# Two of three PReLUs with one ScalarE pass each, and small sums at the ends of PSUM banks, in a fused convolution and attention kernel

## The chip, the cores and the metric

The kernel runs on one core of a Trainium2 chip. A core has five engines that work from queues of their own: TensorE (PE, the matrix multiplier), VectorE (DVE), ScalarE (ACT), GpSimd (POOL) and SyncE (SP), which here issues the DMA transfers. TensorE writes only to PSUM, a small memory of eight banks of 512 fp32 columns on each of 128 partitions. In this kernel VectorE and ScalarE read and write both PSUM and SBUF, and POOL works on SBUF alone. The metric is the time on the device in microseconds (us); lower is better. A profile also records when each instruction ran on each engine.

## What is computed

Input `x` is (16, 256, 56, 56) in fp32. There are two layers, each added to its own input, and each starts with a group norm over 32 groups. Cut to what matters:

```python
# layer 0, on _gn(x)
xq = sign(x + bias)
for i, d in enumerate((1, 3, 5)):                  # three dilations, 4 channel groups
    wq = scale_i * sign(w[i] - mean(w[i]))         # one scale per output channel: mean |w|
    y = conv3x3(xq, wq, dilation=d) + cb[i] - move1[i]
    y = where(y >= 0, y, alpha[i] * y)             # PReLU, one alpha per channel
    out = out + y + move2[i]
out = (out - mean_c(out)) * rsqrt(var_c(out) + eps) * gamma + beta   # over the 256 channels
x = x + out
# layer 1, on _gn(x): 8 heads, 9 neighbours of each pixel
q, k_in, v_in = qkv(x)
k = unfold3x3(k_in) + dcb + dwconv(k_in) + rpb     # v likewise, without rpb
x = x + proj(softmax(q . k over the 9) . v)
```

## The kernel before

The 16 images are worked on one after another, with the stages of neighbouring images overlapping. An image is cut into two strips (`u` = 0, 1), and a strip is held as tiles of 128 partitions by 784 columns (`UNIT`): 64 channels of the upper and 64 of the lower half of the image stand on the partitions. The 256 channels make four groups `g` of 64. So `conv` (line 706) is called 24 times an image: 2 strips x 4 groups x 3 dilations `d`.

**One convolution.** 36 matmuls (line 716) fill one pair of PSUM banks, columns 0 to 391 of each. Then a PReLU is taken from the pair and summed into the strip's tile `ct`. With `c` the sum in PSUM, `s` the weight scale and `b` the bias, PReLU is `alpha*(s*c + b) + (1 - alpha)*relu(s*c + b)`. The part `alpha*s*c` is written or added first: by ScalarE into `ct` for the first dilation (line 735, with the constant `mv2` as its bias), by VectorE into `ct` for the second (line 745), by ScalarE into a tile `rl` for the third (line 742). ScalarE then takes the Relu in place in PSUM (line 750), and VectorE adds `oalpha` times it to `ct` or `rl` (line 755). For the third dilation, POOL at last adds `rl` to `ct` (line 761). The scalars per channel are `asc` (`alpha*s`), `csc` (`s`), `cbi` (`b`) and `oalpha` (`1 - alpha`); `asc` and `csc` are written by `keep` (line 1220) as the weights are prepared, the others by `vectors` (line 1114).

**The channel norm.** `channel_norm` (line 793) squares `ct` on ScalarE (799), sums `ct` and its square over the channels on TensorE (769, in `lanes_sum`, with the constant matrix `cm32`), works out mean and root in small steps (813 to 821), spreads them back by TensorE (783), subtracts the mean (827) and multiplies by the root (837) on VectorE, adds the result to `xt` on POOL (850), and squares again on ScalarE (854) for the second group norm.

**Small sums.** `group_stats` (line 572) serves both group norms: one small matmul chain (587) and some nine small steps on VectorE and ScalarE (599 to 607) in a PSUM pair `gp`. `fold` (866) scales the qkv weights by the result and forms the biases `bf` by small matmuls (884) in a pair `bp`.

**The attention.** qkv (matmuls 906, ScalarE evictions 924); nine products of `q` with shifted rows of `k` (line 959, on POOL or VectorE) into tiles `p`; ten matmul groups (980) that sum them to the scores; the softmax on VectorE and ScalarE (1009 to 1031); for each of nine neighbours a matmul group (1044), a VectorE step (1055) into a tile `m` and a POOL add (1070), and a last VectorE step (1075); the projection (1087) and its VectorE add into `xt` (1097); then the store (1107).

**Who goes first.** Instructions are not issued in the order of the loops. The class `Plan` (line 368) collects them as `Op`s. Each has a place: `PERIOD` times the image, plus a number from the table `ORDER`, which has a row for each stage (`conv0` is strip 0's convolutions; `$` marks the last image's rows, `^` the first's). `Plan.emit` goes by rising place and takes the first operation whose inputs were issued and whose buffers are free; each engine then works through its own queue in that order, and waits where its next instruction's inputs aren't ready. `ON_VECTOR` lists the operations of `either` that VectorE does instead of POOL. The number of buffers of a kind bounds how far the order can run ahead: 4 pairs of PSUM banks (`ps`), 8 `ct`, 1 `rl`, 7 `p`, 4 `m`.

Of the kernel before, what the change touches and what calls it, by code (L numbers as in the profile page):

```python
# [34 lines left out]
LANES = 32  # L35
SCALE = (C // NH) ** -0.5
# [36 lines left out]
class Op:  # L73
    def __init__(self, place, emit, bufs):
# [6 lines left out]
PERIOD = 1231  # L81
ORDER = {
    "conv0": (
        -682, -410, -359, -2832, -303, -327, -265, -333, -280, -264, -245, -1566, -289, -213, -969, -970,
        -319, -128, -2067, -24, -3260, -58, -18, -16, -1028, -3936, 5, 17, 18, 101, 198, -321, 208, -3768,
        197, 207, 182, -601, -3937, 20, -15, -19, -199, 30, -146, 111, -2560, 21, -394, -20, -152, -3331,
    ),
    "conv0$": (
        -685, -409, -2692, -2836, -277, -2837, -419, -253, 194, -189, 109, -866, -1791, -207, -131, -440,
        -4781, -30, -3248, 99, -154, -250, -557, -386, -2111, -2366, 32, -462, -149, -2080, 175, -1794,  # L90
        -2185, -2439, 121, 140, -6017, -1732, -220, -9, -641, 100, -155, 112, -1493, 147, -1733, 191, 240,
        149, -865, -2379,
    ),
    "conv0^": (
        -2099, -6338, -223, -5746, -1337, -3215, -66, -5779, -1241, -202, -65, -5786, -1673, 42, -67, -667,
        -358, 124, 92, 358, -3217, 123, 231, 234, -3216, 565, 167, 400, 401, -1668, 228, 318, 504, -54, 229,
        -13, 515, -1726, -288, 227, 402, -115, -71, 40, -72, 517, -1182, 702, -116, -769, -2031, 119,
    ),
    "conv1": (
        160, -122, -123, 185, 199, -740, 209, -834, 265, -287, 150, -2506, -1087, 320, 171, 170, -823, 333,  # L100
        -2428, 361, -1220, 326, -175, 180, -1339, 356, 319, 255, 254, -2493, 355, -1340, 394, -1221, 714,
        746, 632, -113, -2040, 412, -162, -296, -1322, 470, -3611, 514, -1195, 925, -1683, -2369, 905, -1995,
    ),
    "conv1$": (
        56, -644, -645, -1492, 306, -11476, -498, -11477, 418, 239, 237, -3613, 188, 148, 146, 190, -1497,
        248, -878, 152, -867, 292, 151, -2181, -2390, -2392, 192, 98, 66, -864, 773, -432, 813, -1612, 662,
        456, 455, -1613, -818, 419, -28, -29, 44, 774, -431, 816, -434, 953, 968, 284, 678, -660,
    ),
    "conv1^": (
        666, 513, 523, -1198, 726, -697, -757, 826, 776, 581, 725, 830, 871, 682, 522, 601, -2033, 828, 824,  # L110
        695, 832, 829, 724, 578, 835, 715, 711, 612, 609, -2032, 865, 831, 878, 811, 949, 902, 901, 1044,
        1106, 38, 717, 718, 827, 869, 815, 890, -2027, 922, -1136, -964, 940, 959,
    ),
    "first^": (-3247,),
    "fold": (
        1404, -2035, -892, -2087, -3779, -4755, -952, -4221, -7223, -9967, -564, -942, -953, 1414, -949,
        -562, 1455, 407,
    ),
    "fold$": (
        1238, 1089, 753, 927, 1174, 593, 772, 1298, 934, 929, 595, 268, 1484, 297, 648, 1286, 559, -6518,  # L120
    ),
    "fold^": (
        1395, -941, -2847, -582, -784, 793, 792, -861, -863, -1498, -846, 1074, 1037, 696, 1424, -847, 1481,
        1444,
    ),
    "load0": (310,),
    "load0$": (539,),
    "load0^": (744,),
    "load1": (771,),
    "load1$": (614,),  # L130
    "load1^": (-117,),
    "mean0": (
        301, -2124, -1860, -2389, 172,
    ),
    "mean0$": (
        336, 87, 139, -232, -216,
    ),
    "mean0^": (
        785, 930, 214, -4431, 979,
    ),  # L140
    "mean1": (
        719, 911, 1038, -307, 787,
# [218 lines left out]
    "scale0^": (10,),  # L361
    "scale1$": (4,),
    "scale1^": (4,),
    "value0^": (4,),
}


# [1051 lines left out]
```

## Time and profile before

| | before |
|---|---|
| median of 3 runs | 1863.83 us (1862.01 to 1864.88) |
| the profiled execution: its own time | 1872.31 us |
| its span, first to last instruction | 1870.5 us |
| mean granted TensorE clock | 0.979 |
| instructions | 62125 |
| DMA | 217.03 MB, mean 116 GB/s |
| busy in the first 34 us: PE, DVE, ACT | 10.12, 28.93, 13.17 us |

Times in the profile are in us unless marked ns. Engines: PE is the matmul, PEld the load of its weights, which overlaps it. In a row of a group, after the line, the engine and the operation come the names (output <- inputs), the shapes, the count, and after a bar the busy time with the mean of one in ns, and then the idle time of the engine just before them, with what ended it. A row of waits says who waited for whom, for how long in total, how often, and the longest. The chain of work that ended last is followed back from the last instruction: at each step to what released it, or to the instruction before it on its engine. An idle engine that isn't the bottleneck costs nothing.

### The profile page before, as it was taken

Reading aid. Unit: us, or ns where it says so; the run is one execution under the profiler, and the core shown is the slowest. Engines: PE = TensorE matmul, PEld = TensorE weight load, DVE = VectorE, ACT = ScalarE, POOL = GpSimd, SP = SyncE. Lnnn points to the kernel's source line nnn. Section 1 sums busy time; section 2 is a strip of 40 time slices with the busy share of each in tenths; the row PEclk is TensorE's granted clock in tenths of the full one; section 3 lists DMA queues with packets and bytes.
Section 4 is the critical chain, followed back from the end, with each engine's and each line's share of the span. In section 5 each row is a group of like instructions: output and inputs, shape, how many; then the busy total and the mean of one; then the engine's idle time right before and its main releaser. Section 6 shows DMA issues by size and latency. Waiting matters only on the chain.

```text
span 1870.5 us, 62125 instructions
## 1 busy us (share of the span) xinstructions
PE 1653.7 (88%) x27322; PEld 953.1 (51%) x27322; DVE 1570.8 (84%) x2217; ACT 1314.6 (70%) x1861; POOL 1408.7 (75%) x782
## 2 busy tenths in 40 slices
PE   4879899898999989898998989899898989989784
PEld 3546455454545545454554545455454545745341
DVE  8777979979797997979799797979979797997966
ACT  5988778677777867677786777778677787755320
POOL 2147769688686968868696886869688686967865
PEclk9799999999999999999999999999999999999897
DMA  7852655547475554647555464755547467223023
GB/s 178 200 113 43 143 123 122 126 93 155 96 158 111 124 126 92 149 102 155 115 120 124 96 151 101 156 113 124 123 94 150 101 147 172 62 69 74 11 61 69
DMA packets 102094, 217.03 MB, mean 116 GB/s; under 512 B 10816, under 2 KB 84672, under 8 KB 101568
## 3 DMA queue, kind: packets, MB, share of 16 engines
q1 hardware_dynamic: 101824, 213.06, 51.8%
q8 instruction: 214, 3.51, 0.8%
q14 instruction: 56, 0.46, 0.1%
HBM read 156.23 MB, written 51.38 MB: 111 GB/s over the span
## 4 chain that ended last, share of the span: by engine, by line
PE 53%; POOL 18%; DVE 16%; issue 6%; ACT 4%; DMA 1%; SPq 0%; POOLq 0%; DVEq 0%; ACTq 0%
PE banks L716 19%; POOL m L1070 13%; PE banks L906 12%; PE banks L980 9%; DVE m L1055 4%; PE banks L1044 3%; PE banks L769 3%; POOL xt L850 3%; PE banks L1087 2%; ACT banks L750 2%; DVE rl L755 2%; DVE ct L755 2%; POOL p L959 1%; POOL ct L761 1%; DVE m L1075 1%
## 5 line engine op out<-in xcount | busy, mean ns | idle before, releaser
L716 PE MATMUL banks<-sgn,wconv 64*64 64x392 bf16 x13824 | 656.7, 335 | 60.3 <-DVE m L1055 25.8
L716 PEld LDWEIGHTS <-wconv 64*64 64x64 bf16 x13824 | 442.8, 106 | 279.1 <-issue 94.7
L1070 POOL TENSOR_TENSOR m<-m 128x784 f32<-128x784 f32 x255 | 475.3, 1864 | 95.9 <-DVE m L1055 82.2
L959 POOL TENSOR_TENSOR p<-qt,kt 128x784 f32<-128x784 f32 x267 | 468.1, 1789 | 93.2 <-ACT qt L924 88.0
L750 ACT ACTIVATE banks<-banks,cbi,csc 128x784 f32<-128x784 f32 x384 | 370.3, 973 | 95.8 <-DVE ct L745 95.8
L761 POOL TENSOR_TENSOR ct<-ct,rl 128x784 f32<-128x784 f32 x125 | 233.3, 1866 | 252.7 <-DVE ct L755 147.8
L1044 PE MATMUL banks<-at,wv 64*64 64x392 f32 x2560 | 276.1, 510 | 56.5 <-DVE lv L821 22.6
L1055 DVE SCALAR_TENSOR_TENSOR m<-banks,vb,vt 128x784 f32<-128x784 f32 x288 | 289.6, 1022 | 25.4 <-POOL m L1070 17.6
L755 DVE SCALAR_TENSOR_TENSOR ct<-banks,oalpha,ct 128x784 f32<-128x784 f32 x256 | 258.1, 1026 | 17.1 <-ACT banks L750 16.4
L906 PE MATMUL banks<-xt,wf 64*64 64x392 f32 x3072 | 269.0, 491 | 0.0
L850 POOL TENSOR_TENSOR xt<-xt,ct 128x784 f32<-128x784 f32 x124 | 229.2, 1871 | 1.4 <-DVE ct L837 1.3
L980 PE MATMUL banks<-p,wk 64*64 64x392 f32 x2304 | 213.7, 489 | 2.8 <-POOL p L959 2.6
L742 ACT ACTIVATE rl<-banks,asc 128x784 f32<-128x784 f32 x128 | 116.7, 912 | 107.0 <-PE banks L716 103.0
L906 PEld LDWEIGHTS banks<-xt,wf 64*64 64x64 f32 x3072 | 131.2, 133 | 101.2 <-issue 68.3
L643 ACT ACTIVATE xh<-xh 128x1568 f32<-128x1568 f32 x120 | 180.6, 1507 | 0.7
L735 ACT ACTIVATE ct<-banks,mv,asc 128x784 f32<-128x784 f32 x128 | 128.5, 1004 | 73.0 <-PE banks L716 72.8
L755 DVE SCALAR_TENSOR_TENSOR rl<-banks,oalpha,rl 128x784 f32<-128x784 f32 x128 | 131.8, 1030 | 53.6 <-ACT banks L750 48.8
L1044 PEld LDWEIGHTS banks<-at,wv 64*64 64x64 f32 x2560 | 86.8, 134 | 176.3 <-issue 69.2
L745 DVE SCALAR_TENSOR_TENSOR ct<-banks,asc,ct 128x784 f32<-128x784 f32 x128 | 131.0, 1024 | 24.9 <-PE banks L716 21.3
L980 PEld LDWEIGHTS banks<-p,wk 64*64 64x64 f32 x2304 | 93.1, 133 | 93.4 <-issue 76.2
L854 ACT ACTIVATE ct<-xt,pr 128x784 f32<-128x784 f32 x128 | 120.2, 940 | 25.4 <-POOL xt L850 23.0
L1087 PE MATMUL banks<-m,wp 64*64 64x392 f32 x1024 | 106.4, 518 | 32.1 <-DVE m L1075 29.6
(115 smaller groups left out, 1870.6 us busy)
## 6 DMA issues: line engine op xcount, KB each, us to landing
xh<-in_x SPq DMA_DIRECT2D x248, 392.0 KB, 5.7
xt<-in_x SPq DMA_DIRECT2D x128, 392.0 KB, 9.2
out<-xt SPq DMA_DIRECT2D x128, 392.0 KB, 5.9
sgn<-sgn SPq DMA_DIRECT2D x128, 41.2 KB, 7.6
p<-in_w SPq DMA_DIRECT2D x12, 144.0 KB, 3.2
xt<-in_wk_parts SPq DMA_DIRECT2D x1, 1344.0 KB, 8.1
xt<-in_wv_parts SPq DMA_DIRECT2D x1, 1280.0 KB, 9.4
wq<-in_wqkv SPq DMA_DIRECT2D x1, 384.0 KB, 9.7
```

The costliest lines, as they stand in the source:

```text
L643: lambda func=func, col=col: nc.scalar.activation(inside(g) if b == 0 else image(xh), image(xh), func, accum_out=sums[:, col : col + 1]),
L716: nc.tensor.matmul(out=ps[q * GC : (q + 1) * GC, h, 0:SN], lhsT=wconv[h * GC : (h + 1) * GC, g, d, tap, :], rhs=sgn[g][h * GC : (h + 1) * ...
L750: lambda: nc.scalar.activation(n(), n(), AF.Relu, bias=cbi[:, g, s], scale=csc[:, g, s]),
L755: lambda: nc.vector.scalar_tensor_tensor(to.tile, n(), oalpha[:, g, s], to.tile, ALU.mult, ALU.add),
L761: lambda e: e.tensor_tensor(ct.tile, ct.tile, to.tile, ALU.add),
L850: lambda e, g=g: e.tensor_tensor(xt[:, g], xt[:, g], ct[g].tile, ALU.add),
L906: nc.tensor.matmul(out=ps[h * D : (h + 1) * D, q, 0:SN], lhsT=wf[q * GC : (q + 1) * GC, g, j, :], rhs=xt[q * GC : (q + 1) * GC, g, h, :], ...
L959: e.tensor_tensor(p.tile.rearrange("p x (r w) -> p x r w", w=W), _view(qt[:, 0, u * SN :], [(NU * SN + LANES, 2), (W, SR), (1, W)]), shift ...
L980: nc.tensor.matmul(out=ps[q * D : (q + 1) * D, h, 0:n], lhsT=wk[r, j, :], rhs=rhs, start=s == 0, stop=s == 9,)
L1044: nc.tensor.matmul(out=ps[h * D : (h + 1) * D, q, 0:SN], lhsT=wv[q * D : (q + 1) * D, j, :], rhs=at[q * D : (q + 1) * D, h, 0:SN], start=True,
L1055: lambda j=j, m=m, ps=ps: nc.vector.scalar_tensor_tensor(m.tile.rearrange("p x (r w) -> p x r w", w=W), _view(ps[:, 0, :], [(512, 2), (W, ...
L1070: lambda e, m=m, acc=acc: e.tensor_tensor(acc.tile, acc.tile, m.tile, ALU.add),
```

## The change

For the first and third dilation the size of `1 - alpha` now goes into the Relu's scale and bias. `keep` and `vectors` prepare other scalars: `rsc` in place of `csc` (for these two dilations multiplied by that size), and `sgd`, which is +1 or -1 by the sign of `1 - alpha`. ScalarE takes one Relu pass from PSUM straight into SBUF, and VectorE adds `asc` times the PSUM pair to it. The second dilation keeps its three passes. For the third, ScalarE then makes a pass inside SBUF that brings in `mv2` and the sign; for the first, the sign is brought in later, by the matrix `cms` in the channel sum and by the mean subtraction (line 827), which takes a scalar with it. `rl` has two buffers.

The small sums `gp` and `bp` get a buffer kind of their own, `few`: columns 470 to 511 of the second bank of each pair. All eight banks are now one PSUM tile, and buffers are views of it, handed out in the order in which they came free. The POOL add at 1070 gets a view by rows of its tiles. `ORDER`, `PERIOD` and `ON_VECTOR` have new values throughout.

```diff
+TAIL = 470
-PERIOD = 1231
+PERIOD = 1207
 ORDER = {
...
-    "load1": (771,),
+    "load1": (237,),
...
     "stats": (
-        -1755, -1273, -1265, -1692, -1019, -872, -1573, -996, -832, -1698, -871, -772,
+        -2179, -1470, -1454, -2178, -1363, -1351, -2180, -1288, -1251, -1601, -1248, -2081,
...
 ON_VECTOR = {
-    "conv0$": (12,),
-    "conv1$": (25, 51),
-    "prod0": (5,),
-    "prod0$": (3, 4, 6, 8),
-    "prod0^": (3,),
-    "prod1$": (1, 6),
-    "scale0$": (7,),
-    "scale0^": (10,),
-    "scale1$": (4,),
-    "scale1^": (4,),
-    "value0^": (4,),
+    "conv0$": (23,),
+    "prod0": (6,),
+    "prod0$": (2, 4, 6, 8),
+    "prod0^": (3, 4, 5),
+    "prod1": (2, 6),
+    "prod1$": (1, 3),
+    "scale0$": (1,),
+    "scale1$": (7,),
 }
...
-        self.free = {k: n for k, (_, n) in self.kinds.items()}
+        self.views = {k: list(v) for k, v in self.kinds.items() if isinstance(v, list)}
+        self.free = {k: len(v) if isinstance(v, list) else v[1] for k, v in self.kinds.items()}
...
-                    b.tile = self.kinds[b.kind][0]()
+                    b.tile = self.views[b.kind].pop(0) if b.kind in self.views else self.kinds[b.kind][0]()
...
-    psum = ctx.enter_context(tc.tile_pool(name="psum", bufs=4, space=bass.MemoryType.PSUM))
+    psum = ctx.enter_context(tc.tile_pool(name="psum", bufs=1, space=bass.MemoryType.PSUM))
+    banks = psum.tile([P, 8, 512], F32, name="banks")
...
-    kinds = {"ps": (banks, 4)}
+    kinds = {
+        "ps": [banks[:, 2 * i : 2 * i + 2] for i in range(4)],
+        "few": [banks[:, 2 * i + 1 : 2 * i + 2, TAIL:512] for i in range(4)],
+    }
...
-    kind("rl", UNIT, 1)
+    kind("rl", UNIT, 2)
...
-        gp, e, v, m2 = Buf("ps"), Buf("g"), Buf("g"), Buf("g")
+        gp, e, v, m2 = Buf("few"), Buf("g"), Buf("g"), Buf("g")
...
         to = Buf("rl") if d in POOLED else ct
-        if d == 0:
-            act(
-                lambda: nc.scalar.activation(
-                    ct.tile, n(), AF.Identity, bias=mv2[:, g : g + 1], scale=asc[:, g, s]
-                ),
-                [ps, ("scales", g, d), "mv2"],
-                [ct],
-            )
-        elif d in POOLED:
-            act(lambda: nc.scalar.mul(to.tile, n(), asc[:, g, s]), [ps, ("scales", g, d)], [to])
-        else:
+        stt = nc.vector.scalar_tensor_tensor
+        if d == 1:
             dve(
-                lambda: nc.vector.scalar_tensor_tensor(ct.tile, n(), asc[:, g, s], ct.tile, ALU.mult, ALU.add),
+                lambda: stt(ct.tile, n(), asc[:, g, s], ct.tile, ALU.mult, ALU.add),
...
         act(
-            lambda: nc.scalar.activation(n(), n(), AF.Relu, bias=cbi[:, g, s], scale=csc[:, g, s]),
-            [("scales", g, d)],
-            [ps],
+            lambda: nc.scalar.activation(
+                n() if d == 1 else to.tile, n(), AF.Relu, bias=cbi[:, g, s], scale=rsc[:, g, s]
+            ),
+            [("scales", g, d)] if d == 1 else [ps, ("scales", g, d)],
+            [ps] if d == 1 else [to],
         )
...
+        if d == 1:
+            dve(lambda: stt(ct.tile, n(), oalpha[:, g, s], ct.tile, ALU.mult, ALU.add), [ps], [ct])
+        else:
+            dve(
+                lambda: stt(to.tile, n(), asc[:, g, s], to.tile, ALU.mult, ALU.add),
+                [ps, ("scales", g, d)],
+                [to],
+            )
+        if d == 2:
+            act(
+                lambda: nc.scalar.activation(
+                    to.tile, to.tile, AF.Identity, bias=mv2[:, g : g + 1], scale=sgd[:, g, 2:3]
+                ),
+                ["mv2"],
+                [to],
+            )
...
-                lanes_sum(ps, 0, ct[g], g)
-                lanes_sum(ps, 1, sq, g)
+                lanes_sum(ps, 0, ct[g], g, cms[:, g, :])
+                lanes_sum(ps, 1, sq, g, cm32)
...
-                lambda g=g: nc.vector.tensor_tensor(ct[g].tile, ct[g].tile, mb[:, :, 0:SN], ALU.subtract),
+                lambda g=g: stt(
+                    ct[g].tile, ct[g].tile, sgd[:, g, 0:1], mb[:, :, 0:SN], ALU.mult, ALU.subtract
+                ),
...
-        bp, bf = Buf("ps"), Buf("g")
+        bp, bf = Buf("few"), Buf("g")
...
-                        lambda e, m=m, acc=acc: e.tensor_tensor(acc.tile, acc.tile, m.tile, ALU.add),
+                        lambda e, m=m, acc=acc: e.tensor_tensor(
+                            *(t.tile.rearrange("p x (r w) -> p x r w", w=W) for t in (acc, acc, m)), ALU.add
+                        ),
...
+        nc.vector.tensor_scalar(sgd, oalpha, 0.0, 2.0, ALU.is_ge, ALU.mult)
...
-                nc.vector.tensor_scalar(csc[:, g, s], tp[:, 1, 256:257], 1.0 / (GC * 9), None, ALU.mult)
-                nc.vector.tensor_tensor(asc[:, g, s], csc[:, g, s], alpha[:, g, s], ALU.mult)
+                nc.vector.tensor_tensor(rsc[:, g, s], rho[:, g, s], tp[:, 1, 256:257], ALU.mult)
+                nc.vector.tensor_tensor(asc[:, g, s], sal[:, g, s], tp[:, 1, 256:257], ALU.mult)
```

`vectors` gains 13 small VectorE instructions for these scalars, of which the one above is an example, and the step that finishes `mv2` one.

## The prediction

> **What bounds the kernel now.** I read the page's shares first, then the chain that ended last for the rhythm, then the busy time in stretches, then the waits.
>
> ```profile
> PE 1653.7 (88%) x27322; PEld 953.1 (51%) x27322; DVE 1570.8 (84%) x2217; ACT 1314.6 (70%) x1861; POOL 1408.7 (75%) x782
> ```
>
> Four engines lie within 18 points of one another, so no share alone names the bound. The chain, in order of time, repeats with the image:
>
> ```profile
> 366.14 4.77 PE banks L716 x95
> ...
> 1567.10 4.77 PE banks L716 x96
> ```
>
> The same piece comes back after 11 images: (1567.10 - 366.14) / 11 = 109.2 us per image. Sixteen of those are 1747 us; the other 123 us are head and tail. One period in two halves and whole (the columns are length, PE, PEld, DVE, ACT, POOL, granted clock, DMA share, GB/s), and then a stretch of the head:
>
> ```profile
> 803.27:857.00 53.73, 53.73 (x911) 30.79 (x914) 40.38 (x68) 42.47 (x63) 40.47 (x24) 1.00 0.48 107
> 857.00:912.06 55.06, 46.46 (x792) 26.27 (x788) 53.26 (x65) 39.51 (x55) 47.71 (x26) 1.00 0.64 139
> 803.27:912.06 108.79, 100.19 (x1695) 57.05 (x1698) 93.63 (x132) 81.98 (x117) 88.18 (x49) 1.00 0.56 123
> ```
>
> ```profile
> 34.00:150.00 116.00, 89.92 (x1669) 58.33 (x1672) 89.53 (x158) 101.34 (x135) 32.74 (x17) 0.88 0.69 156
> ```
>
> The first half (qkv, scores, convolutions) is TensorE's without a gap, with 13.4 us of VectorE idle. The second half (attention values, norms, convolutions) is VectorE's, 53.26 of 55.06 us, and there TensorE loses 8.6 us. In the head ScalarE is the fullest. What TensorE waits for in that period:
>
> ```profile
> PE banks L716 <- DVE m L1055: 2.0, 2, 1.1
> PE banks L1087 <- DVE m L1075: 1.6, 1, 1.6
> PE banks L1044 <- DVE lv L821: 1.6, 1, 1.6
> PE banks L716 <- DVE ct L837: 1.1, 1, 1.1
> PE banks L1044 <- DVE rl L755: 0.8, 1, 0.8
> ```
>
> All are waits for VectorE, nearly all for a PSUM pair that VectorE has yet to read. No row names a DMA. The prices come from these groups:
>
> ```profile
> L1070 POOL TENSOR_TENSOR m<-m 128x784 f32<-128x784 f32 x255 | 475.3, 1864 | 95.9 <-DVE m L1055 82.2
> L959 POOL TENSOR_TENSOR p<-qt,kt 128x784 f32<-128x784 f32 x267 | 468.1, 1789 | 93.2 <-ACT qt L924 88.0
> L750 ACT ACTIVATE banks<-banks,cbi,csc 128x784 f32<-128x784 f32 x384 | 370.3, 973 | 95.8 <-DVE ct L745 95.8
> L837 DVE SCALAR_TENSOR_TENSOR ct<-ct,pr,banks 128x784 f32<-128x784 f32 x128 | 124.2, 1024 | 1.1 <-PE banks L783 0.3
> L742 ACT ACTIVATE rl<-banks,asc 128x784 f32<-128x784 f32 x128 | 116.7, 912 | 107.0 <-PE banks L716 103.0
> L735 ACT ACTIVATE ct<-banks,mv,asc 128x784 f32<-128x784 f32 x128 | 128.5, 1004 | 73.0 <-PE banks L716 72.8
> L854 ACT ACTIVATE ct<-xt,pr 128x784 f32<-128x784 f32 x128 | 120.2, 940 | 25.4 <-POOL xt L850 23.0
> ```
>
> **ScalarE.** For one channel group of one strip it now runs L735 once, L742 once and L750 three times: 1004 + 912 + 3 x 973 = 4835 ns. Afterwards: two Relus from PSUM to SBUF with two per-partition scalars (L735's form, 1004 each), one L750, and for the third dilation an Identity inside SBUF. No row has that last form; between L854's 940 (one scalar) and 1100, I take 940 plus the 92 that L735 costs over L742: 1032. Together 4013, so -822 ns, eight times an image: -6.6 us of its 82. That ends no steady period by itself, since ScalarE idles 27 us in each.
>
> What matters is how long a pair of banks is held. For two of three convolutions it was two ScalarE passes and a VectorE pass (3.0 us) and becomes one and one (2.0). In the period shown this bears on two waits: L1044 behind L755's `rl` (0.8), which itself waited for L742 and L750, and one of the two L716 waits (1.0), for an L1055 that VectorE started only after that `rl`. I count -1.8. Bounds: 0, if the freed pair is at once awaited behind another VectorE pass, to -3.4 (the two rows behind L755 and L1055, and L769's 0.6). The new Identity waits for VectorE, and behind it on ScalarE stand the next evictions, while the POOL add L761 waits for it; ScalarE's 27 us and the second `rl` buffer cover that. Where they don't, it costs up to 1.0 us a time.
>
> **VectorE.** Its number of passes over the convolutions is unchanged. The mean subtraction L827 becomes the scalar form: 961 to L837's 1024, eight times, +0.5 us. `ON_VECTOR` puts three products an image on VectorE where there was one: +2 x 1.25 us (the mean of L959 on VectorE). Together +3.0 us: 96.6 in a period. Where these fall in the first half, VectorE's idle time there hides them; the products of strip 1 lie at its end, where VectorE has under 1 us free in 9, so I let 40% through: +1.2. Bounds 0 and +3.0.
>
> Here a rule speaks against the change. In the trace, L959 on VectorE has a median of 0.98 us and a longest of 2.49. The Trainium skill, "SBUF — State Buffer", section "SBUF: two separate sides", says that a VectorE operation with two SBUF inputs and a GpSimd operation reading SBUF exclude each other for a whole instruction. Most of the traced ones started while POOL stood idle for the same `qt`; products 2 and 6 lie amid POOL's own. By the rule each would wait half a POOL product, 0.9 us, and hold POOL for 0.98. VectorE's addition is then 4.8, not 3.0, and POOL's relief 1.6, not 3.6. I take the row for the forecast and the rule for a rival.
>
> **POOL.** Two products fewer: -2 x 1.79 = -3.6 us of 88. It opens the accumulations L1070 earlier, which are 17% of the period's chain, and the L1087 wait (1.6) ends on the last of them. I take -1.0; bounds 0 and -1.6. The adds L1070 get the row-wise access pattern that L959 has. L959 is 75 ns shorter, but a product; the bounds are 0 and -75 ns, and half, over the ten adds on the chain, is -0.4.
>
> **Small sums.** Statistics and biases no longer take a pair of their own. In the period they fall at 803 and 810 to 812 us, where TensorE has no gap, and at 850, the same: 0 gained. What sharing a bank costs is a rival below.
>
> **New places.** Every queue is re-sorted. SP's loads and stores move past one another too (`load1` 771 to 237, `stats` -1755 to -2179); with no wait for a DMA in the period and a DMA share of 0.56 I price them at nothing, up to some 6 us each time should a load come late (an `xh` load lands in 5.7). For the order itself no row exists: from -6 us a period (TensorE alone left) to +3 (a worse fit); I take 0.
>
> **Head and tail.** ScalarE is 101.34 of 116 us in the head; half of image 0's 6.6 us shows: -3.3. `vectors` gets 13 more small instructions, at 0.19 us (L1124's three take 0.56) 2.5 us on a chain that is VectorE's from 12.8 us; about 1 us of that hides behind the first load: +1.5. The tail has ScalarE at 127 of 304 us: 0, within 8 either way.
>
> **The sum.** A period: -1.8 + 1.2 - 1.0 - 0.4 = -2.0 us. Fourteen (the first and last image are priced apart): -28.0; head -1.8; together -29.8. The profiled execution took 1872.31 us (span 1870.5 and 1.8 around it), so 1842.5. The median of the timed runs, 1863.83, is 0.9955 of it: 1834.
>
> **The rivals.** *VectorE becomes the bound* (20%). All of its 3.0 us land in the second half: -0.2 a period, 1859. By the lock rule 4.8, and POOL gives 0.4: +2.2 a period, 1893. For it: 53.26 of 55.06 us. Against: 13.4 us idle in the first half. It turns to a loss once more than 3.2 us of added VectorE time reach the second half. I centre it at 1872.
>
> *The shared bank makes TensorE wait* (17%), the rival for slower. The row says nothing is paid: past the head, TensorE waits some 3 us before L587 in the whole run. The Trainium skill, "PSUM — Partial Sum Buffer", section "PSUM bank collisions raise a hardware error", says to guard PSUM by bank and quadrant, not by address. So a small sum at columns 470 to 511 must wait until the pair's convolution has been read, and the next convolution there until the small chain (2.2 us in the fold at 803 us) is through. A convolution's matmuls and two passes last 3.6 us; half, three times an image, is +5.4 a period. Against -2.0: +3.4, 14 times, less the head's 1.8: 1909. It decides from 0.7 us for each small sum. A paid 1.5 gives 1897.
>
> *TensorE alone* (12%): the new order closes most gaps, 103.5 us a period against 100.2 busy, -5.7 x 14: 1783.
>
> *The change doesn't do what it says* (3%, slower): the pass inside SBUF delays the POOL add and gives back what the banks gained.
>
> **How the numbers follow.** The forecast's case has 48%, from 1815 to 1853 (1.4 us a period either way, 14 times). About 0.2% (3.7 us) is what a measurement of this kernel tells from no change. Faster: 48 + 12 + 6 of the VectorE rival = 66%. Same: 5 of it. Slower: 9 of it, 17 and 3 = 29%. The range takes in the forecast's case, the VectorE rival and most of the other two: 1790 to 1890.
>
> **What would show it.** Right: ScalarE near 1210 us, VectorE near 1615, POOL near 1350; the period near 107; L1044 no longer behind L755's `rl`; L1087's wait shorter. Wrong: TensorE idle before L587 or L884 for an eviction (shared bank); VectorE products of 1.9 us (lock); a second half with VectorE at 55 of 55; a DMA named as releaser.

## The result: 8 to 9% slower, and the profile after

The kernel after takes 2036.66 us (median of four runs, 2013.10 to 2060.13), the kernel before 1862.92 beside it. The ratio is 1.0825, interval 1.0786 to 1.0865; since the kernel after scatters by 2%, this rests on its two faster runs (2013.10 and 2020.77), and the profiled execution, 2052.55 us, is one of the two slower, so that its sums lie some 36 us above them. The prediction was 1834 with a range to 1890: wrong in sign and far outside.

First the busy row of the profile:

```profile
PE 1740.0 (85%) x27322; PEld 1022.9 (50%) x27322; DVE 1658.3 (81%) x2256; ACT 1227.2 (60%) x1733; POOL 1384.2 (68%) x757
```

ScalarE fell by 87 us, as meant, and POOL by 25. TensorE runs the same 27322 matmuls and is busy 86.3 us longer. The span grew from 1870.5 to 2049.7; less TensorE's busy time that leaves 216.8 us of idle TensorE before and 309.7 after. So the loss in this execution has two halves of like size: 86 us in which the same matmuls run more slowly, and 93 us more in which TensorE waits.

The new groups show that the single passes cost what was expected. L748 is the Relu, L764 the pass inside SBUF, L1083 the POOL add with the view by rows, L972 the products on VectorE:

```profile
L748 ACT ACTIVATE ct<-banks,cbi,rsc 128x784 f32<-128x784 f32 x128 | 128.1, 1003 | 215.6 <-PE banks L723 215.6
L764 ACT ACTIVATE rl<-rl,mv,sgd 128x784 f32<-128x784 f32 x128 | 131.5, 1031 | 14.2 <-DVE rl L758 14.0
L1083 POOL TENSOR_TENSOR m<-m 128x784 f32<-128x784 f32 x256 | 476.8, 1862 | 94.6 <-DVE m L1068 82.8
L972 DVE TENSOR_TENSOR p<-qt,kt 128x784 f32<-128x784 f32 x51 | 119.3, 2345 | 53.1 <-ACT qt L937 50.5 <-PE banks L993 2.6
```

Only the last is off: 2345 ns a product in the mean, where before the mean was 1249 (and the median 976). The view by rows gained nothing, 1862 against 1864 ns.

The busy time in stretches, one of the shortest and one of the longest periods (same columns as before: length, PE, PEld, DVE, ACT, POOL, granted clock, DMA share, GB/s):

```profile
1233.50:1346.00 112.50, 102.30 (x1696) 60.92 (x1690) 97.38 (x134) 76.53 (x109) 86.55 (x48) 0.98 0.54 119
869.88:1001.25 131.37, 110.01 (x1696) 64.65 (x1690) 106.98 (x134) 76.33 (x109) 84.36 (x48) 0.90 0.47 102
```

Before, a period was 109.2 us. Now it is 112 to 136, on average 121.9 (the 2.8 us wait at the values' matmuls comes back once an image, first at 358.58 us and after 12 images at 1820.9). Over 14 periods, 14 x 12.7 = 178 us: nearly the whole growth of the span (179.2), so head and tail hardly matter. In the longer period the granted clock is 0.90 and the same 1696 matmuls take 8 us more. What TensorE waits for in the whole run, first the longest rows before, then after:

```profile
PE banks L1087 <- DVE m L1075: 29.6, 16, 6.9
PE banks L716 <- DVE m L1055: 25.8, 26, 1.1
PE banks L1044 <- DVE lv L821: 22.6, 14, 2.0
```

```profile
PE banks L919 <- DVE banks L1022: 37.7, 4, 9.6
PE banks L1057 <- DVE ct L838: 37.2, 13, 3.5
PE banks L723 <- DVE g L609: 21.3, 9, 3.1
PE banks L594 <- DVE m L1068: 15.7, 6, 3.0
PE banks L919 <- DVE g L907: 14.6, 5, 3.1
```

The waits of before that the prediction worked with are gone: the values' matmuls (L1044, now L1057) wait 1 us behind `rl`, the projection (L1087, now L1102) 6.0 us against 29.6. In their place stand fewer and longer ones. The first row after is four waits of over 9 us for qkv's banks. The second comes once an image: the pair for the values is still being read by the four mean subtractions. Between 250 and 1850 us, counted in the timeline, TensorE had 4 gaps of 2.2 us or more before, 14.6 us together; after, 34, 125 us together. The shorter gaps in that stretch fell from 125 to 72 us. No load is to blame: TensorE waits for a DMA once in the whole run, 1.6 us, and the other engines four times, 26 us together.

What follows a gap, here one of the values' waits, is seen in the timeline of TensorE, and in the stretches of 2 us around it (the clock is the third column from the right):

```profile
834.97 1.73 PE L723 MATMUL banks<-sgn,wconv 64*64 64x392 bf16 x36
839.51 3.74 PE L1057 MATMUL banks<-at,wv 64*64 64x392 f32 x24 [2.81 <-DVE ct L838]
```

```profile
836.00:838.00 2.00, 0.70 (x18) 0.24 (x8) 2.00 (x3) 1.23 (x2) 1.63 (x1) 1.00 1.03 265
838.00:840.00 2.00, 0.49 (x4) 0.30 (x8) 2.00 (x3) 1.96 (x4) 0.29 (x1) 0.78 1.06 225
840.00:842.00 2.00, 2.00 (x16) 0.45 (x8) 1.50 (x3) 1.97 (x3) 1.57 (x1) 0.50 1.01 219
842.00:844.00 2.00, 1.60 (x16) 0.54 (x16) 1.73 (x4) 2.00 (x3) 0.42 (x1) 0.87 0.29 63
```

A gap of 2.81 us, then some 3.4 us at half the clock: 16 matmuls fill 2 us there. Of the 34 gaps above, 32 are followed by a stretch at half the clock that begins within 4 us of the gap's end. The mean granted clock of the run is 0.928, and was 0.979. So such a gap is paid twice: as idle time, and by about 1.7 us (half of 3.4) for matmuls behind it.

### The profile page after: what moved, and what is told of

Its sections match the earlier page's. It is cut to its first block, busy times and chain, and to the rows that moved or that the text cites. A ratio compares the mean times of both kernels' runs of the same rounds, so it can differ in the third digit from the quotient of the medians.

```text
span 2049.7 us, 61850 instructions
## 1 busy us (share of the span) xinstructions
PE 1740.0 (85%) x27322; PEld 1022.9 (50%) x27322; DVE 1658.3 (81%) x2256; ACT 1227.2 (60%) x1733; POOL 1384.2 (68%) x757
## 4 chain that ended last, share of the span: by engine, by line
DVE 42%; PE 35%; issue 10%; POOL 6%; ACT 5%; DVEq 0%; DMA 0%; POOLq 0%; SPq 0%; ACTq 0%
PE banks L723 11%; PE banks L919 10%; DVE m L1068 6%; DVE ct L838 5%; PE banks L993 4%; PE banks L1057 4%; DVE ct L850 4%; DVE ct L743 4%; DVE rl L758 3%; DVE ct L758 3%; POOL p L972 3%; DVE xt L1112 2%; PE banks L1102 2%; DVE p L972 2%; POOL m L1083 2%
## 5 line engine op out<-in xcount | busy, mean ns | idle before, releaser
L1083 POOL TENSOR_TENSOR m<-m 128x784 f32<-128x784 f32 x256 | 476.8, 1862 | 94.6 <-DVE m L1068 82.8
L772 POOL TENSOR_TENSOR ct<-rl,ct 128x784 f32<-128x784 f32 x127 | 237.1, 1872 | 436.8 <-DVE banks L668 141.2
L972 POOL TENSOR_TENSOR p<-qt,kt 128x784 f32<-128x784 f32 x237 | 424.0, 1831 | 88.0 <-PE banks L993 44.8
L919 PE MATMUL banks<-xt,wf 64*64 64x392 f32 x3072 | 318.3, 542 | 52.3 <-DVE banks L1022 37.7
L1057 PE MATMUL banks<-at,wv 64*64 64x392 f32 x2560 | 289.1, 551 | 61.5 <-DVE ct L838 37.2
L748 ACT ACTIVATE ct<-banks,cbi,rsc 128x784 f32<-128x784 f32 x128 | 128.1, 1003 | 215.6 <-PE banks L723 215.6
L919 PEld LDWEIGHTS banks<-xt,wf 64*64 64x64 f32 x3072 | 161.7, 146 | 176.2 <-issue 80.1
L743 DVE SCALAR_TENSOR_TENSOR ct<-banks,asc,ct 128x784 f32<-128x784 f32 x128 | 130.9, 1025 | 121.9 <-PE banks L723 121.6
L748 ACT ACTIVATE banks<-banks,cbi,rsc 128x784 f32<-128x784 f32 x128 | 124.5, 973 | 149.9 <-DVE ct L743 149.1
L1057 PEld LDWEIGHTS banks<-at,wv 64*64 64x64 f32 x2560 | 90.5, 142 | 194.1 <-DVE m L1068 60.8
L748 ACT ACTIVATE rl<-banks,cbi,rsc 128x784 f32<-128x784 f32 x128 | 127.7, 998 | 75.9 <-PE banks L723 62.1
L758 DVE SCALAR_TENSOR_TENSOR rl<-banks,asc,rl 128x784 f32<-128x784 f32 x128 | 131.3, 1027 | 42.1 <-ACT rl L748 41.5
L972 DVE TENSOR_TENSOR p<-qt,kt 128x784 f32<-128x784 f32 x51 | 119.3, 2345 | 53.1 <-ACT qt L937 50.5
L755 DVE SCALAR_TENSOR_TENSOR ct<-banks,oalpha,ct 128x784 f32<-128x784 f32 x128 | 131.5, 1029 | 26.8 <-ACT banks L748 22.3
```

The lines of the kernel that those rows point to most:

```text
L743: lambda: stt(ct.tile, n(), asc[:, g, s], ct.tile, ALU.mult, ALU.add),
L748: lambda: nc.scalar.activation(n() if d == 1 else to.tile, n(), AF.Relu, bias=cbi[:, g, s], scale=rsc[:, g, s]),
L758: lambda: stt(to.tile, n(), asc[:, g, s], to.tile, ALU.mult, ALU.add),
L772: lambda e: e.tensor_tensor(ct.tile, to.tile, ct.tile, ALU.add),
L919: nc.tensor.matmul(out=ps[h * D : (h + 1) * D, q, 0:SN], lhsT=wf[q * GC : (q + 1) * GC, g, j, :], rhs=xt[q * GC : (q + 1) * GC, g, h, :], ...
L972: e.tensor_tensor(p.tile.rearrange("p x (r w) -> p x r w", w=W), _view(qt[:, 0, u * SN :], [(NU * SN + LANES, 2), (W, SR), (1, W)]), shift ...
```

## The experiments

The theories. A: VectorE's products are held back by POOL, the rival of the lock. B: the small sums in shared banks make TensorE wait. C: the new PReLU itself costs, by its extra pass. D: the new places open the gaps, whatever the instructions are. All figures are medians, with the ratio to the kernel before, measured alongside (1862 to 1870 us), and its interval.

### Undoing the products and the shared banks

```diff
 ON_VECTOR = {
-    "prod0": (6,),
-    "prod1": (2, 6),
```

> The kernel after, with the products of the 14 middle images all on POOL (the rows prod0 and prod1 of ON_VECTOR removed, places unchanged). Theory A (a VectorE product that falls into a run of POOL instructions is locked out until that run has a gap: four of 11 us and some twenty of about 1 us extra in the profile, each followed by a TensorE gap and a lower granted clock): VectorE's L972 falls from 119 to under 20 us, no instruction of it over 3 us, and the time falls by 60 to 90 us, to about 1940. Theory B (small sums sharing a bank are the main loss): it falls by under 20 us, since POOL gets 42 products of 1.73 us more. Theory C (the new places lose by themselves): within 20 us of the kernel after.

```diff
-        gp, e, v, m2 = Buf("few"), Buf("g"), Buf("g"), Buf("g")
+        gp, e, v, m2 = Buf("ps"), Buf("g"), Buf("g"), Buf("g")
-        bp, bf = Buf("few"), Buf("g")
+        bp, bf = Buf("ps"), Buf("g")
```

> The kernel after, with the small sums gp and bp in a pair of banks of their own again (kind ps instead of few), places unchanged. Theory B (sharing a bank makes TensorE wait before L594, L897 and behind L609 and L907, some 85 us of idle in the profile): those waits go, time falls by 50 to 90 us. Theory A: the waits go but the lock-out of the products stays, time falls by under 30 us. If a pair of its own is scarce under these places, other TensorE waits for a pair take their place and the time rises.

Both edits together:

> Both: products of the middle images on POOL and small sums in pairs of their own; what is left of the change is the PReLU, the row view of the POOL adds, and the places. If A and B explain the loss together: 1860 to 1900 us, with a granted clock of 0.97 or more. If the places lose by themselves (C): over 1940.

| kernel | us | ratio | interval |
|---|---|---|---|
| after, products on POOL | 2038.3 | 1.0945 | 1.0920 to 1.0969 |
| after, sums in pairs of their own | 2047.73 | 1.0987 | 1.0952 to 1.1022 |
| after, both | 2047.78 | 1.0986 | 1.0966 to 1.1006 |

None gives anything back, so neither A nor B is the loss of this kernel. With both undone the period is a steady 122.2 us, so even without a single product on VectorE in the middle images every period is 13 us too long. Without the products the runs also scatter less (2037 to 2045 against 2013 to 2060), which fits with the long products, four in the profiled run, falling now here and now there; that was not tested further. B falls outright: on top of the first edit, giving the sums their own pairs costs 9.5 us.

### The PReLU alone, at the old places

The edit is the PReLU of the change, cut here to the third dilation's Relu and its new pass:

```diff
         act(
-            lambda: nc.scalar.activation(n(), n(), AF.Relu, bias=cbi[:, g, s], scale=csc[:, g, s]),
+            lambda: nc.scalar.activation(to.tile, n(), AF.Relu, bias=cbi[:, g, s], scale=rsc[:, g, s]),
...
+        if d == 2:
+            act(lambda: nc.scalar.activation(to.tile, to.tile, AF.Identity, bias=..., scale=...), ["mv2"], [to])
```

The Identity pass has no old place; it got that of the VectorE step just ahead of it.

> The kernel before, with only the PReLU of the first and third dilation changed (and two rl buffers); places of before, the dropped ScalarE pass's place left out, the new pass inside SBUF at the place of the VectorE step. If the PReLU by itself is worth what was forecast (banks held 1 us less): 1835 to 1850 us. If ScalarE was never in the way: 1860 to 1866. If the pass inside SBUF delays POOL: over 1870.

It took 2052.81 us (1.102, 1.0995 to 1.1046). ScalarE's waits name the reason; L748 is the Identity, L742 the VectorE step, L732 the Relu:

```profile
ACT rl L748 <- DVE rl L742: 234.2, 117, 5.5
ACT rl L732 <- PE banks L707: 153.6, 87, 12.7
```

The Identity stands in ScalarE's queue 128 times, and 117 times ScalarE stops there for VectorE, 2.0 us each, with the next evictions behind it. To see whether this is the whole of it, the same kernel without the pass:

```diff
-            act(lambda: nc.scalar.activation(to.tile, to.tile, AF.Identity, bias=..., scale=...), ["mv2"], [to])
+            act(lambda: None, ["mv2"], [to])
```

> The kernel before with the new PReLU for the first and third dilation at the old places, as in the run of the PReLU alone (2052.8), but without the added Identity pass (the last offset and the sign of the third dilation are left out). If the Identity pass, which ScalarE must hold back until VectorE has finished the step before it, carries the loss: 1820 to 1870, and ScalarE no longer waits 234 us for VectorE's rl. If the new PReLU costs for another reason (the first pass writes the SBUF and VectorE's product comes after it): 1950 to 2050.

1873.38 us (1.0045, 1.0029 to 1.0062), 3 us above what was expected if the pass is the whole of it. The new PReLU without its third-dilation pass costs next to nothing, and the pass right behind VectorE costs 179 us. Next the pass was put later in ScalarE's order. VectorE's order is that of the run at 2052.8 but for one pair of instructions, and TensorE's is the same as far as the trace tells; POOL's changes, since its add comes after the pass:

```diff
-            o = next((o for o in todo if not o.wait and self.room(o)), None)
+            o = next((o for o in todo if not o.wait and o.due <= acts and self.room(o)), None)
...
+                x.due = acts + x.late        # late = 3 for the Identity pass, 0 for all others
```

> The kernel before with the whole new PReLU at the old places, Identity pass included, as in the run of the PReLU alone (2052.8), with one difference: the Identity pass is put into ScalarE's order three ScalarE steps after the VectorE step that it needs, not right behind it. TensorE's and VectorE's orders are those of that run. If the loss of that run was ScalarE waiting in order for VectorE (234 us of waits for rl): 1865 to 1900, near the 1873 of the same kernel without the pass, and the whole PReLU edit is then worth about nothing, so that the loss of the change lies in its places. If the pass itself is too dear: over 1950.

> The whole new PReLU at the old places with the Identity pass one ScalarE step after the VectorE step that it needs (none: 2052.8; three: 1940.6, where the channel sums on TensorE waited 31 us for POOL's addition, which comes after the pass). If the pass costs by blocking ScalarE's queue alone: between the two, 1960 to 2020. If it costs by lengthening the way from the bank to POOL's addition, and a shorter lag is better for that: below 1940.

| Identity pass | us | ratio | ScalarE waits at it | TensorE waits for POOL's add |
|---|---|---|---|---|
| none | 1873.38 | 1.0045 | - | 3.0 us |
| right behind VectorE | 2052.81 | 1.102 | 234.2 us | 4.0 |
| one step later | 1951.19 | 1.0443 (1.0416 to 1.0471) | 86.5 | 32.1 |
| three steps later | 1940.57 | 1.0417 (1.0382 to 1.0452) | 1.7 | 34.3 |

The lag of three takes ScalarE's wait away, but not the cost. Against the run without the pass TensorE is idle 36 us longer and busy 38 us longer, at a mean clock of 0.963 against 0.979. The idle part is seen in TensorE's waits with that lag, where L772 is the channel sum and L764 POOL's add; the second row was 25.6 us without the pass, the first 3.0:

```profile
PE banks L772 <- POOL ct L764: 34.3, 15, 2.9
PE banks L714 <- DVE m L1060: 31.2, 26, 5.5
```

The pass lengthens the way from the banks to POOL's add, and the last add of a strip is what the channel sum waits for. My expectation for the lag of three, 1865 to 1900, was wrong: behind the first price stood a second. The lag of one, 1951, fell between its two expectations (1960 to 2020, or below 1940): a blocked queue and the longer way both count. C holds at the old places: the pass costs 67 us where it is placed best here.

### The same pass, under the new places

```diff
-            act(lambda: nc.scalar.activation(to.tile, to.tile, AF.Identity, bias=..., scale=...), ["mv2"], [to])
+            act(lambda: None, ["mv2"], [to])
```

> The kernel after without the added Identity pass (the last offset and the sign of the third dilation are left out), all else as after. If the Identity pass carries the loss under the new places too: 1850 to 1900. If the new places carry it: 2000 to 2050, little less than 2037, since the pass is 8 x 1.03 = 8.2 us of ScalarE a period and ScalarE has slack there. If both: near 1950.

2055.94 us (2024.64 to 2067.82, where the kernel after had 2013.10 to 2060.13): no better than after. This fits the profile after: by the row of L764 above ScalarE waits for VectorE only 14.0 us in the whole run, and TensorE never waits for POOL's add, L772. C isn't the loss of the kernel after.

### The places alone

The run at 1873 and the next one differ in the list of places and in which operations VectorE takes from POOL: 17 of its operations, 12 of them products, go to POOL. The instructions are otherwise the same.

```diff
-PERIOD = 1231
+PERIOD = 1207
 ORDER = {
...
-    "mean1": (719, 911, 1038, -307, 787,),
+    "mean1": (982, -1898, -1896, -1897, -1899,),
...
```

> The kernel of the run with the new PReLU and no Identity pass at the old places (1873.4), with one thing changed: the new list of places, and with it the new choice of the steps that VectorE takes (its rows for the products of inner images left out). The instructions are otherwise the same; the last offset and the sign of the third dilation are left out in both. If the places alone carry the loss of the change: 2020 to 2060, TensorE idle near 15 us a period beside 9. If the loss needs the Identity pass, the products or the shared banks: 1865 to 1900.

2048.88 us (1.0969, 1.0933 to 1.1004). This is D, and the size is the whole loss: 2048.9 - 1873.4 = 175.5 us, where the medians of after and before differ by 173.7. The busy rows, old places and then new:

```profile
PE 1648.9 (88%) x27322; PEld 947.7 (51%) x27322; DVE 1574.8 (84%) x2231; ACT 1110.7 (59%) x1605; POOL 1408.6 (75%) x782
```

```profile
PE 1737.9 (85%) x27322; PEld 1031.6 (50%) x27322; DVE 1567.7 (77%) x2214; ACT 1110.9 (54%) x1605; POOL 1427.1 (70%) x799
```

ScalarE does the same work in both, VectorE 7 us less. TensorE's busy time grows by 89.0 us (its clock goes from 0.979 to 0.944) and its idle time by 85.0 (from 222.7 to 307.7): the two halves of the loss of the kernel after, from another order. (The 17 operations were not moved alone at the old places. TensorE waits for a product of POOL's 3.3 us in this whole run, and for no other work of POOL's.) The waits of the new order (L532 is the convolution, L860 the values, L641 the mean subtraction, L567 VectorE's step on `rl`):

```profile
PE banks L532 <- DVE rl L567: 37.9, 33, 2.9
PE banks L860 <- DVE ct L641: 34.8, 13, 3.5
PE banks L532 <- DVE m L871: 28.6, 20, 2.3
```

The values' wait behind the mean subtractions is that of the kernel after (37.2 us, 13 times). In the old list the four subtractions of the second strip have places spread from -307 to 1038, and in the new one all four have places below -1895, which puts them into VectorE's queue as early as their input allows, one behind the other.

The old PReLU at the new places, which were not made for it (the middle images' products are all on POOL here, unlike in the kernel before):

> The kernel before with nothing but the new list of places (each step of the old PReLU that has no row of its own in the new list takes the row of the step beside it) and two rl buffers; products as before, small sums in pairs of their own, PReLU as before. If the new places carry the loss (the order of steps opens gaps of over 2 us at TensorE, and the clock drops behind them): 2010 to 2060, TensorE idle about 15 us a period beside 8.6 before. If the places are sound and the loss comes from the new PReLU: within 1% of 1863, 1850 to 1885. In between, both carry a part.

2121.83 us (1.1379, 1.1351 to 1.1407): worse again, and above the 2010 to 2060 expected.

Which half of the list does it? Two mixed lists, with small sums in pairs of their own and one product an image on VectorE, as before; in the second the Identity pass has its lag of three:

> The kernel after with products and small sums undone (2047.8 in that form), and the old places for the attention half (fold, qkv, products, scores, softmax, values, projection) beside the new ones for the first half (loads, statistics, signs, convolutions, channel norm), period 1231. If the loss sits in the new attention places: 1870 to 1920. If it sits in the new places of the first half: 2030 to 2080. If an order is good only as a whole: over 2050 here and in the run with the halves swapped.

> The other way round: the old places for the first half (with the Identity pass three ScalarE steps late, as in the run of that name) and the new ones for the attention half, period 1231, products and small sums undone. If the loss sits in the new places of the first half: 1870 to 1920. If in those of the attention half: 2030 to 2080. If an order is good only as a whole: over 2050.

2376.66 us (1.2749, 1.2712 to 1.2785) and 2317.67 (1.2440, 1.2409 to 1.2472). Both are far worse than either whole list, so the loss can't be put into one half in this way: each half was ordered around the other. The new waits are of other kinds, in the second kernel these among them: a convolution (L549) that stands waiting for its own input, and the channel sum (L607) for POOL's add:

```profile
PE banks L549 <- ACT sgn L500: 74.5, 13, 6.3
PE banks L607 <- POOL ct L599: 60.5, 16, 7.2
```

### Is the clock a cause?

In the kernel with products and small sums undone, the gaps stand at the same points in each period. Two of them, 2.2 and 2.7 us, come just behind a convolution, and that convolution was issued twice:

```diff
+        def twice():
+            for _ in range(2 if d == 0 and u == 0 and g < 2 and 0 < b < NB - 1 else 1):
+                products()
-        pe(products, ...)
+        pe(twice, ...)
```

> The kernel after with products and small sums undone (2047.8 in that form), and work added: two convolution groups of an image (first dilation, first and second channel group) issue their 36 matmuls twice, 1.73 us more of TensorE each, just ahead of the two gaps of 2.2 and 2.7 us that stand in each period there. The result is the same. If a gap of over 2 us costs TensorE half its clock for 3.4 us afterwards: the gaps shrink to 0.5 and 1.0 us, two drops a period go, 2 x 1.7 us x 13 periods = 44 us less, about 2004, with more work done. If the clock is no cause: unchanged at 2048, or up to 45 us more where the added matmuls delay others.

2040.24 us (1.0946, 1.0918 to 1.0975), against 2047.78 (1.0986, 1.0966 to 1.1006) without the added work. Its busy row, and ahead of it that of the kernel without:

```profile
PE 1737.6 (85%) x27322; PEld 1033.6 (51%) x27322; DVE 1566.7 (77%) x2214; ACT 1221.4 (60%) x1733; POOL 1428.1 (70%) x799
```

```profile
PE 1754.5 (86%) x28330; PEld 1053.3 (52%) x28330; DVE 1563.8 (77%) x2214; ACT 1223.6 (60%) x1733; POOL 1427.9 (70%) x799
```

There are 1008 more matmuls, 28 x 1.73 = 48.4 us of them, yet TensorE is busy only 16.9 us longer: the others run 31.5 us faster, and the mean clock rises from 0.945 to 0.963. The work added had to cost 48 us or be hidden in the gaps; 25.5 us were hidden, 31.5 came back through the clock, and the kernel is 7.5 us quicker by the medians (the two intervals overlap by a little, so it is at least no slower for the added work). So the clock is a cause of its own, though no run shows how many of its 86 us in the kernel after would come back with it. The forecast of 44 us less was too much: it let the gaps swallow all of the added work, and they swallowed half.

### Products alone, and the first dilation alone, at the old places

```diff
 ON_VECTOR = {
-    "prod0": (5,),
+    "prod0": (6,),
+    "prod1": (2, 6),
```

> The kernel before with three products of an image's query and key on VectorE in place of one, as after has them, nothing else changed. If the prediction's price is right (3.0 us more on VectorE a period for two products of 0.98 us and the wait, 40% of it through): 14 x 1.2 = 17 us more at most, 1863 to 1885. If VectorE's products are held back by POOL's run of products (the 12 us products of after): over 1900.

1945.33 us (1.0405, 1.0371 to 1.0439): A is dear here. The timeline of VectorE and POOL, and of the convolution that waits (L717):

```profile
746.41 3.70 POOL L851 TENSOR_TENSOR xt<-xt,ct 128x784 f32<-128x784 f32 x2
747.89 6.51 DVE L960 TENSOR_TENSOR p<-qt,kt 128x784 f32<-128x784 f32 x1
750.04 1.74 POOL L960 TENSOR_TENSOR p<-qt,kt 128x784 f32<-128x784 f32 x1
751.71 1.85 POOL L851 TENSOR_TENSOR xt<-xt,ct 128x784 f32<-128x784 f32 x1
756.35 3.15 PE L717 MATMUL banks<-sgn,wconv 64*64 64x392 bf16 x36 [5.64 <-DVE ct L756]
756.37 1.87 POOL L762 TENSOR_TENSOR ct<-ct,rl 128x784 f32<-128x784 f32 x1 [2.80 <-DVE ct L756]
```

A product of 0.98 us lasts 6.51. POOL goes on without a gap to 753.56; the product ends at 754.40, about one product's time later. POOL stops there because its own next instruction (L762) waits for VectorE, so here the hold lasts until POOL has nothing left that it can do without VectorE. It was so in 9 of the 14 middle images, with 6.2 to 6.5 us each time and the same wait of 2.80 us at L762. In four others the product got in behind one instruction of POOL's and took 1.2 us, from the same start within POOL's run:

```profile
635.43 4.41 POOL L851 TENSOR_TENSOR xt<-xt,ct 128x784 f32<-128x784 f32 x2
636.91 1.23 DVE L960 TENSOR_TENSOR p<-qt,kt 128x784 f32<-128x784 f32 x1
```

What decides between the two is open. The kernel after shows the hold in a longer run of POOL's, which ends at 560.14:

```profile
546.09 7.36 POOL L863 TENSOR_TENSOR xt<-xt,ct 128x784 f32<-128x784 f32 x4
553.34 6.80 POOL L972 TENSOR_TENSOR p<-qt,kt 128x784 f32<-128x784 f32 x4
```

```profile
548.99 11.98 DVE L972 TENSOR_TENSOR p<-qt,kt 128x784 f32<-128x784 f32 x1
```

```profile
562.94 4.38 PE L919 MATMUL banks<-xt,wf 64*64 64x392 f32 x32 [9.22 <-DVE banks L1022]
```

Behind that product VectorE's transpose of the scores, L1022, comes late, and qkv's banks with it: these are the four waits of over 9 us. Only these four products are held so long; the other 27 that start while POOL is in a run take 0.99 to 2.50 us.

The last: one ScalarE pass fewer for each group, and no pass added (the constant of the first dilation's pass goes into the third's as its bias, and the sign is left out).

```diff
         if d == 0:
-            act(lambda: nc.scalar.activation(ct.tile, n(), AF.Identity, bias=mv2[...], scale=asc[...]), ...)
-            act(lambda: nc.scalar.activation(n(), n(), AF.Relu, bias=cbi[...], scale=csc[...]), ...)
+            act(lambda: nc.scalar.activation(ct.tile, n(), AF.Relu, bias=cbi[...], scale=rsc[...]), ...)
```

> The kernel before, with the new PReLU for the first dilation only: one ScalarE pass fewer for each group of a unit (8 a period, 2 x 4), no pass added; the channel's last offset is the bias of the third dilation's scaling pass, which costs nothing; the sign for 1-alpha below 0 is left out. Old places, the removed step's place dropped. If ScalarE's sum counts for the first half as the prediction had it: 8 passes x about 1.0 us = 8 us of ScalarE a period off, ScalarE 120 us less over the run, and the time 1835 to 1860. If ScalarE was never the limit at these points: within 0.3% of 1863. If the order of steps is so tight that any shift opens gaps: over 1890.

1879.9 us (1.0073, 1.0046 to 1.0100): 0.7% slower, with 97 us of ScalarE's work gone, and in none of the ranges expected. No version here beat the kernel before.

## Why the prediction was wrong, by its own steps

**"New places ... I take 0", bounds -6 and +3 a period.** This is the step that failed. The measured term, at the same instructions but for the 17 that changed engines, is 175.5 / 14 = +12.5 us a period. It was called a term without a row and then given narrow bounds around zero, on the ground that TensorE alone limits the gain. The bound on the loss had no ground at all. The kernel before waits for VectorE in many pieces of 0.8 to 1.6 us; another order with equal sums can join these into fewer of 2 to 3, and that is what happened: the gaps of 2.2 us or more went from 14.6 to 125 us, the shorter ones from 125 to 72.

**The clock.** No step priced it: a period was summed as busy time at the clock of before. Half of the span's growth (86 of 179 us) is the same matmuls at a lower clock. The Trainium skill, "TensorE: Matmul & The Clock Gate", section "HAM oscillation — how this bites in real kernels", advises against idle gaps of over about 3.4 us. Here 2.81 us were enough, and in one period of the kernel with both edits undone four gaps of 1.4 to 2.7 us were each followed by half speed. By the rule only 6 of the 34 long gaps, those of over 3.4 us, would count, an estimated 0.8 us a period (6 x 1.7 / 13); by the trace it is some 6 us (86 / 14).

**Held banks, -1.8 a period.** The pair is released one pass earlier, and it brought nothing: at the old places +0.5% for both dilations and +0.7% for the first alone, both at places made for the old passes. The wait for `rl` that should have gone was 10.1 us over the run before, and is 11.2 without the Identity. The lower bound, 0, was the answer.

**The Identity, covered by ScalarE's 27 idle us and the second `rl` buffer, at most 1.0 us a time.** At the old places it cost 179 / 128 = 1.4 us a time right behind VectorE, and 67 / 128 = 0.5 with a lag of three. Idle time in the sum is no cover: the queue is worked off in order, so an instruction that waits takes the idle time from those behind it. In the kernel after ScalarE waits at it 14.0 us, and leaving it out gained nothing.

**VectorE, +1.2 through of +3.0; the lock as a rival at up to +2.2 in all.** At the old places the products alone cost 1945.3 - 1870.1 = 75 us, 5.4 a period. The rule that the prediction quotes from the Trainium skill, "SBUF — State Buffer", section "SBUF: two separate sides", which I weighed and set aside, had the right sign. My reading of it, a wait of half a POOL product, fits the products that took 1.2 to 2.5 us; it missed those that POOL's next instructions went ahead of, 9 of the 21 that start in a run of POOL's here, at 6.2 to 6.5 us. The median of 0.98 in the row came from products that start while POOL stands idle. Under the new places the products' removal gained nothing: the costs of the parts don't add.

**POOL and the row view, -1.4.** POOL was forecast near 1350 and is 1384; the view gave 0.

**Small sums 0, and the shared bank as a rival at +5.4.** The step held and the rival fell: the sums' own pairs were no faster.

**ScalarE's sum** was right: 1227 us where about 1210 was forecast, the new pass at 1031 ns where 1032 was estimated. It was not what the time hung on. **Head and tail** together moved by about 1 us, if the growth of the span is set against 14 mean periods.

Still open: which steps of the new list are to blame. The mean subtractions in a row are the most regular wait, 2.8 us an image, but moving them alone wasn't tried; the mixed lists say only that the halves don't part. How short a gap still brings the clock down isn't settled either. Of the gaps of 1.25 to 2.2 us between 250 and 1850 us, 1 of 28 was followed by half speed within 4 us in the kernel before, and 20 of 26 with both edits undone, so length alone doesn't decide; in the period of the kernel before between 690 and 800 us, a gap of 1.07 us, a 0.9 us group of matmuls behind one of 0.79, was followed by half speed, and one of 2.00 wasn't.

## What to carry to other kernels

In a kernel whose engines all stand near 80%, the issue order is a cost of its own, and of the largest size here: 9% at nearly equal instructions. Price a re-sorted order by the longest gap that it can open at TensorE, count such a gap at its length and half the slow stretch behind it, and if no row shows it, leave the range wide to the bad side. When a pass is taken off an engine that isn't the bound, don't count on a gain (here it was none); when one is added behind another engine's step, look at what stands behind it in the queue.

## What the runs showed of the hardware that I had not expected

- A VectorE product with two SBUF inputs, started in the middle of a gap-free run of POOL's, either gets in behind one POOL operation (1.2 us at 636.91) or is held until about the run's end: 6.51 us at 747.89, 11.98 us in the longest case, where 0.98 is its own time. With the products alone 9 of 21 such products were held, in the kernel after 4 of 31.
- After the TensorE gap of 2.81 us at 836.7 the granted clock is at 0.50 for about 3.4 us. Issuing 1008 more matmuls ahead of two gaps of 2.2 and 2.7 us an image made the remaining ones 31.5 us faster.
- A row-wise view of the POOL add's operands changes nothing: 1862 against 1864 ns.
